# Context keys and values by seven block products per pair of chunks, in a decoder layer in f32

## The chip, the cores and the metric

The kernel runs on one core of a Trainium2 chip. Its metric is the device time of one execution in microseconds, lower is better. The engines are TensorE (PE, matrix products; PEld is its weight load), VectorE (DVE), ScalarE (ACT), GpSimd (POOL) and the queue that issues most transfers (SP). They run side by side, each through its own list of instructions in order, and wait for one another by semaphores.

## The reference

All arrays are f32. `x` has 8 batches of 112 tokens of width 512, the context 8 batches of 375 rows of width 512. Three parts follow one another, each closed by `x = layernorm(x + part(x))`:

```
1. self-attention, 16 heads of 128, causal
2. cross-attention without softmax, 16 heads of 32, f(a) = a + 1 if a > 0 else exp(a):
     q = f(x @ Wq.T);  gate = sigmoid(x @ Wg.T + bg)
     k, v = split(ctx @ Wkv.T);  k = f(k)            # 375 x 512 each, per batch
     summary = sum over context of k v^T;  ksum = sum over context of k
     attn = (q @ summary) / (q . ksum + 1e-6)
     part = (attn * gate) @ Wo.T
3. mixture of 8 experts, top 2 per token, clamped gated unit of width 512
```

The change concerns the line of `k` and `v`: 3000 context rows times a matrix of 512 x 1024.

## The kernel before, in words

The width 512 is cut into `C = 4` blocks of 128 that lie on partitions, and the 896 tokens into 7 tiles of 128. Weights come by 1 MB transfers into nine buffers `slab[0]` to `slab[8]` (three more are added in the last part). PSUM has two groups of four banks, "mm" and "aux"; `bank` hands out the next one, which waits until the last reader of what was in it is done.

**Self-attention** (to 452 us). Per head, `seven` (L279) makes queries and keys of both halves of the tokens with seven block products in place of eight: one accumulator `pa` is read out by ACT three times in the middle of its accumulation (L303, L307, L310), while PE works on another bank. The sums of weights that this needs are made on POOL (L274), where the causal mask of the softmax (L400) runs too.

**Cross-attention** (452 to 748 us). A context of 375 rows is three chunks of `SC = 125`. `load_context` (L690) brings one batch's context, transposed, into one of two buffers `cT`. `project_context(b, sc, n)` (L699) makes the keys (`n = 0`) or values (`n = 1`) of one chunk by four matmuls of 125 x 512 (L704). For keys, DVE takes the minimum with 0 out of PSUM (L713), ACT the exp (L714) and DVE puts the two branches of `f` together (L721); for values, ACT copies them out (L717). `summarize` (L725) sums over the three chunks and masks the result on DVE (L745, L748); `attend` (L751) multiplies with the queries (`dps`, `nps`) and has DVE divide (`z`, with a reciprocal, L768) and multiply into `gate`.

The keys and values of batch 0 are made ahead of the loop, then the queries and gates of all tokens (L789). The loop over batches (L922) makes those of batch `b + 1` while it summarizes batch `b`. Between them it calls `tick` (L667), which moves the open *chains* on by one piece each. A chain is a generator whose `yield` ends a piece: `close(t)` (L866) projects token tile `t` out and adds it (`xops`, L236), normalizes it, and routes it to experts (`x2T`, `lps`, `cps`, scatter into `store`); `keep_scores` (L573) then prepares the tile's first sum (`sTps`, `dbps`, a store into `total`). Within the loop the order of PE, DVE, ACT and SP is the order of the program text; POOL's is planned by the framework, as is everything ahead of the loop. After tile 4 and tile 5 `list_blocks` (L603) makes lists of token blocks for the experts on DVE, and `fetch_weights` / `fetch_tokens` start the transfers for the first steps; step `s` has its weights in slabs `3q` to `3q + 2` with `q = s mod 4`, its biases in `biases[:, q]`.

**Experts** (748 us on). 21 steps of one block of 128 tokens: two products `gups` (L975), sigmoid and clamps, transposes (`aT`, `bT`, L891), one product `yps` (L1001), with weights fetched up to four steps ahead. The chain of tile 6 runs in the first steps.

Of the kernel before, what the change touches and what calls it, by code (L numbers as in the profile page):

```python
# [2 lines left out]

# [6 lines left out]
F32 = mybir.dt.float32  # L10
# [34 lines left out]
def decoder_layer(ctx: ExitStack, tc: tile.TileContext, t_in: dict, out: bass.AP):  # L45
# [182 lines left out]
        nc.scalar.activation(tmp, tmp, AF.Exp)  # L228
        nc.vector.scalar_tensor_tensor(dst, ps, 0.0, tmp, ALU.max, ALU.add)

    def project_and_add(aT, w, tag: str, tiles=range(NT)):

        for t in tiles:
            ps = bank(f"{tag}_{t}")
            for c in range(C):
                nc.tensor.matmul(  # L236
                    ps,
                    aT[:, c, t * P : (t + 1) * P],
                    w[:, c, :],
                    start=(c == 0),  # L240
                    stop=(c == C - 1),
                )
            nc.vector.tensor_add(xn[:, t, :], xn[:, t, :], ps)  # L243
            yield t
# [257 lines left out]
    def route(t: int):  # L502
# [29 lines left out]
            both, expert, i2[:, 1:2], first, ALU.is_equal, ALU.add  # L532
        )
        yield

        cps = bank(f"cps_{t}", "aux")
        nc.tensor.matmul(cps[:, :E], before, both, start=True, stop=True)
# [35 lines left out]
    def keep_scores(t: int, first, both):  # L573

        sco = small.tile([P, E], F32, tag="sco", name=f"sco_{t}")
        yield
        nc.vector.tensor_scalar_mul(sco, both, xe[:, t, XS : XS + 1])
        nc.vector.scalar_tensor_tensor(
            sco, first, xe[:, t, XD : XD + 1], sco, ALU.mult, ALU.add
        )  # L580
        yield
        yield
        sps = bank(f"sTps_{t}", "aux")
        nc.tensor.matmul(sps[:E, :P], sco, ident, start=True, stop=True)
        sT = small.tile([E, P], F32, tag="sT", name=f"sT_{t}", bufs=2)
        nc.scalar.copy(sT, sps[:E, :P])
        yield
        dps = bank(f"dbps_{t}", "aux")
        nc.tensor.matmul(dps, sT, db, start=True, stop=True)  # L589
        first_sum = side.tile([P, D], F32, tag="sum", name=f"sum_{t}")  # L590
        nc.vector.tensor_add(first_sum, xn[:, t, :], dps)
        put = nc.sync.dma_start(out=total[t * P : (t + 1) * P, :], in_=first_sum)
        if t == NT - 1:
            tc.declare_no_dep(put.ins, group="early", reason="tokens of other tiles")
# [81 lines left out]
            tick()  # L676

    with tc.tile_pool(name="cross", bufs=2) as cr:
        wkv = [weights("wkv", 0, 6), weights("wkv", 1, 7)]
        bg = const.tile([P, C], F32, name="bg")  # L680
        nc.sync.dma_start(out=bg, in_=t_in["bg"])
        kv = {}

        values = [
            cr.tile([SC, NSC, C, P + 1], F32, name=f"values{i}", bufs=1) for i in range(2)
# [4 lines left out]
        def load_context(b: int):  # L690
            cT = cr.tile([P, C, SC * NSC], F32, tag="cT", name=f"cT_{b}")
            nc.sync.dma_start(
                out=cT, in_=t_in["ctxT"][b].rearrange("(c p) s -> p c s", p=P)
            )
            kf = cr.tile([SC, NSC, 512], F32, tag="kf", name=f"kf_{b}")
            vs = values[b % 2]
            kv[b] = (cT, kf, vs)

        def project_context(b: int, sc: int, n: int):  # L699

            cT, kf, vs = kv[b]
            ps = bank(f"kvps_{b}_{sc}_{n}")
            for c in range(C):
                nc.tensor.matmul(  # L704
                    ps[:SC, :],
                    cT[:, c, sc * SC : (sc + 1) * SC],
                    wkv[n][:, c, :],
                    start=(c == 0),
                    stop=(c == C - 1),
                )  # L710
            if n == 0:
                tmp = cr.tile([SC, 512], F32, tag="tmp", name=f"kt_{b}_{sc}")
                nc.vector.tensor_scalar_min(tmp, ps[:SC, :], 0.0)  # L713
                nc.scalar.activation(tmp, tmp, AF.Exp)  # L714
                kv[b, sc] = ps, tmp
            else:
                nc.scalar.copy(  # L717
                    vs[:, sc, :, :P], ps[:SC, :].rearrange("p (g e) -> p g e", g=C)
                )
                ps, tmp = kv[b, sc]  # L720
                nc.vector.scalar_tensor_tensor(  # L721
                    kf[:, sc, :], ps[:SC, :], 0.0, tmp, ALU.max, ALU.add
                )

        def summarize(b: int):  # L725

            _, kf, vs = kv[b]
            bdkv = cr.tile([P, C, P], F32, tag="bdkv", name=f"bdkv_{b}")
            bdks = cr.tile([P, C, P], F32, tag="bdks", name=f"bdks_{b}")
            mask = bdmask.unsqueeze(1).broadcast_to([P, 2, P])  # L730
            for i in range(2):
                ps = bank(f"sumps_{b}_{i}", "aux")
                sums = ps[:, : 2 * (P + 1)].rearrange("p (g e) -> p g e", g=2)
                for j in range(2):
                    g = 2 * i + j
                    for sc in range(NSC):
                        nc.tensor.matmul(  # L737
                            sums[:, j, :],
                            kf[:, sc, g * P : (g + 1) * P],
                            vs[:, sc, g, :],  # L740
                            start=(sc == 0),
                            stop=(sc == NSC - 1),
                        )
                pair = slice(2 * i, 2 * i + 2)
                nc.vector.tensor_mul(  # L745
                    bdks[:, pair, :], mask, sums[:, :, P:].broadcast_to([P, 2, P])
                )
                nc.vector.tensor_mul(bdkv[:, pair, :], mask, sums[:, :, :P])  # L748
            return bdkv, bdks
# [20 lines left out]
            nc.vector.tensor_mul(gate[:, :, rows], gate[:, :, rows], z)  # L770

        load_context(0)
        for sc in range(NSC):
            for n in range(2):
                project_context(0, sc, n)
        wxq, wxg = weights("wxq", 0, 4), weights("wxg", 0, 5)
        wxo = weights("wxo", 0, 8)
        xT = keep.tile([P, C, T], F32, tag="xT", name="x1T")
        for _ in transposing(xT, "x1T"):
# [3 lines left out]
        for n, w in (("xq", wxq), ("xg", wxg)):  # L783
            for g in range(C):
                for half in range(2):
# [13 lines left out]
                    else:  # L799
                        nc.scalar.activation(  # L800
                            gate[:, g, cols], ps[:, :HALF], AF.Sigmoid, bias=bg[:, g : g + 1]
                        )
        biases = keep.tile([P, NQ, 2 * I], F32, tag="xT", name="biases")
        blocks = store.rearrange("(n p) w -> n p w", p=P)
        inside = "clamped where it is computed"

# [58 lines left out]

        def close(t: int):  # L866

            for _ in project_and_add(gate, wxo, "xops", (t,)):
                layernorm(t, "ln2")
            yield  # L870
            yield
            first_both = yield from route(t)
            if t == LISTS[0][0] - 1:
                list_blocks(0)
                ahead_w.extend(fetch_weights(s) for s in range(2))
                ahead_x.extend(fetch_tokens(s) for s in range(LISTS[0][1]))
            elif t == LISTS[1][0] - 1:
                list_blocks(1)
                ahead_x.append(fetch_tokens(LISTS[0][1]))
            elif t == NT - 1:  # L880
                list_blocks(2)
            later.append(keep_scores(t, *first_both))
# [33 lines left out]
            st["late"] = s - (STEPS - LATE)  # L916
            return st

        load_context(1)
        ahead_w, ahead_x = [], []  # L920
        in_order = ctx.enter_context(tc.manual_schedule(engines=ORDERED))
        for b in range(B):  # L922
            more = b + 1 < B
            if more:
                project_context(b + 1, 0, 0)
                tick()
            else:
                steps = [start(0, side, "bT")]
                third = fetch_in_parts(2)
                ahead_w.append(next(third))  # L930
                tick()
            sums = summarize(b)
            tick()
            if more:
                project_context(b + 1, 0, 1)
                tick()
            attend(b, *sums, qf, gate)
            tick()
            if more:
                project_context(b + 1, 1, 0)  # L940
                tick()
            if b == LISTS[0][0]:
                chains.append(close(b - 1))
                tick()
            if more:
                project_context(b + 1, 1, 1)
                tick()
            if 0 < b < B - 1 and b != LISTS[0][0]:
                chains.append(close(b - 1))
                tick()  # L950
            if more:
                for n in range(2):
                    project_context(b + 1, 2, n)
                    tick()
            if b + 2 < B:
                load_context(b + 2)


    with tc.tile_pool(name="moe", bufs=2, reuse_waits="tile") as moe:
# [163 lines left out]
        for s in range(STEPS + 1):  # L1123
# [11 lines left out]
            if s + 1 < STEPS:  # L1135
                steps.append(start(s + 1, moe, "bT"))
                if s + 1 > STEPS - LATE:
                    nc.vector.tensor_scalar_mul(diag, ident, keys[:, s + 1 : s + 2])
                if s == 1 or s > STEPS - LATE + 1:
                    tick()  # L1140
                if s == 2:
                    settle(0)
                if s >= 1 and s + 3 < STEPS:
                    ahead_x.append(fetch_tokens(s + 3))
# [85 lines left out]
```

## Time and profile before

| | |
|---|---|
| median of 3 runs | 1013.89 us (1012.16 to 1017.29) |
| the profiled execution's own time | 1014.17 us |
| its span, first to last instruction | 1012.6 us |
| PE / DVE / ACT / POOL busy | 982.3 / 435.2 / 231.8 / 140.9 us |
| granted PE clock | 0.995 |

The page is of one execution. It gives each engine's busy time, the span in 40 slices of 25.3 us (each digit is a share in tenths), the chain of work that ended last, and the costliest groups of instructions: line, engine, operation, output and inputs with shapes, count, then busy us and mean ns of one, then the idle time of the engine ahead of them and what ended it. Other answers of the trace give waits (who waited for whom: us in total, times, longest), the timeline (start us, us, engine, line, operation, the idle time before it in brackets) and the busy time in a stretch. Numbers like L704 are lines of the kernel before.

### The profile page before, as it was taken

The numbers are of one execution on the slowest core, as the hardware profiler recorded it, in microseconds if no ns is written. First come the engines' busy times: TensorE is split into PE (matmuls) and PEld (weight loads), VectorE is DVE, ScalarE is ACT, GpSimd is POOL, SyncE is SP. The second block draws the span as 40 slices with busy tenths as digits, with TensorE's granted clock in tenths as the row PEclk, the third lists the DMA queues.
The fourth block names the chain that finished last, engine by engine and source line by source line (L and its number), as shares of the span: only waits on it lengthen the run. The fifth ranks groups of instructions, "written<-read, shape, count | busy, mean of one in ns | idle before, by whom it ended". The sixth has DMA issues, their size and how long they took to land.

```text
span 1012.6 us, 9328 instructions
## 1 busy us (share of the span) xinstructions
PE 982.3 (97%) x3319; PEld 513.5 (51%) x3319; DVE 435.2 (43%) x988; ACT 231.8 (23%) x406; POOL 140.9 (14%) x183
## 2 busy tenths in 40 slices
PE   7998999999999999999999999999999999999995
PEld 3455544566446655645555555554554444444442
DVE  1356511255124533563314455544676343334384
ACT  1132311133003312312221212122113211121132
POOL 3134200023002211000000000000111212111132
PEclk9999999999999999999999999999999999999998
DMA  8990004111010201110001010111668896692342
GB/s 334 359 347 17 1 1 166 42 42 42 0 42 1 83 0 42 43 61 30 1 0 31 1 63 21 62 42 62 235 264 348 323 388 209 197 342 44 94 95 70
DMA packets 33837, 114.98 MB, mean 114 GB/s; under 512 B 3845, under 2 KB 8005, under 8 KB 26240
## 3 DMA queue, kind: packets, MB, share of 16 engines
q1 hardware_dynamic: 26784, 98.28, 26.4%
q0 software_dynamic: 6336, 15.75, 6.3%
q8 instruction: 26, 0.43, 0.2%
q10 hardware_dynamic: 672, 0.36, 0.1%
q14 instruction: 19, 0.16, 0.0%
HBM read 115.83 MB, written 29.01 MB: 143 GB/s over the span
## 4 chain that ended last, share of the span: by engine, by line
PE 90%; DVE 3%; issue 3%; ACT 1%; DMA 1%; POOL 1%; POOLq 0%; ACTq 0%; DVEq 0%
PE kvps L704 16%; PE gups L975 12%; PE ops L236 10%; PE yps L1001 6%; PE vps L326 6%; PE zps L434 3%; PE xops L236 2%; PE xqps L789 2%; PE xgps L789 2%; PE sps L386 2%; PE sumps L737 2%; PE pps L426 1%; PE dbps L589 1%; PE aT_ps L891 1%; PE bT_ps L891 1%
## 5 line engine op out<-in xcount | busy, mean ns | idle before, releaser
L704 PE MATMUL kvps<-slab,cT 128*125 128x512 f32 x384 | 170.4, 594 | 0.0
L975 PE MATMUL gups<-slab,bT 128*128 128x512 f32 x336 | 151.3, 593 | 0.0
L704 PEld LDWEIGHTS kvps<-slab,cT 128*125 128x125 f32 x384 | 70.4, 188 | 82.9 <-issue 81.3
L236 PE MATMUL ops<-slab,zT 128*128 128x512 f32 x224 | 97.9, 593 | 0.0
L975 PEld LDWEIGHTS gups<-slab,bT 128*128 128x128 f32 x336 | 62.0, 190 | 69.5 <-issue 68.6
L1001 PE MATMUL yps<-slab,aT 128*128 128x512 f32 x168 | 77.6, 606 | 4.1 <-ACT aT L895 4.1
L983 DVE TENSOR_TENSOR gu<-gups,biases 128x512 f32<-128x512 f32 x42 | 29.0, 691 | 118.4 <-PE gups L975 118.3
L236 PEld LDWEIGHTS ops<-slab,zT 128*128 128x128 f32 x224 | 42.0, 190 | 50.3 <-issue 49.3
L326 PE MATMUL vps<-slab,x0T 128*112 128x512 f32 x128 | 59.2, 618 | 1.0 <-DVE x0T L186 0.8
L274 POOL TENSOR_TENSOR ws<-slab 128x256 f32<-128x256 f32 x16 | 11.8, 736 | 316.0 <-PE qk_5c L290 83.0
L562 POOL DMA_INDIRECT store<-xn,rows x14 | 13.8, 985 | 299.6 <-DVE xn L560 242.1
L1001 PEld LDWEIGHTS yps<-slab,aT 128*128 128x128 f32 x168 | 31.9, 194 | 43.4 <-issue 37.6
L1015 POOL DMA_INDIRECT total<-y,nums x19 | 30.4, 1599 | 129.4 <-ACT y L1012 117.5
L713 DVE TENSOR_SCALAR kt<-kvps 125x512 f32<-125x512 f32 x24 | 16.5, 689 | 67.4 <-PE kvps L704 67.4
L243 DVE TENSOR_TENSOR xn<-xn,ops 128x512 f32<-128x512 f32 x28 | 19.2, 686 | 56.1 <-PE ops L236 56.1
L434 PEld LDWEIGHTS zps<-pT,v 112*128 112x128 f32 x256 | 33.5, 192 | 12.3 <-issue 11.2
L326 PEld LDWEIGHTS vps<-slab,x0T 128*112 128x112 f32 x128 | 23.0, 185 | 31.7 <-issue 30.0
L441 DVE COPY zT<-zps 128x448 f32<-128x448 f32 x32 | 20.0, 624 | 39.8 <-PE zps L434 39.8
L434 PE MATMUL zps<-pT,v 112*128 112x112 f32 x256 | 33.4, 273 | 0.0
L714 ACT ACTIVATE kt<-kt 125x512 f32<-125x512 f32 x24 | 15.1, 630 | 78.4 <-DVE kt L713 73.7
L410 DVE TENSOR_REDUCE nm<-p 112x4 f32<-112x448 f32 x32 | 19.7, 616 | 30.8 <-POOL p L400 30.8
L1012 ACT COPY y<-yps 128x512 f32<-128x512 f32 x20 | 11.7, 585 | 92.0 <-issue 81.4
(569 smaller groups left out, 1387.7 us busy)
## 6 DMA issues: line engine op xcount, KB each, us to landing
slab<-in_wg_dram SPq DMA_DIRECT2D x21, 1024.0 KB
slab<-in_wu_dram SPq DMA_DIRECT2D x21, 1024.0 KB
slab<-in_wd_dram SPq DMA_DIRECT2D x21, 1024.0 KB
store<-slab SPq DMA_DIRECT2D x8, 1806.0 KB
biases<-gubs SPq DMA_DIRECT2D x21, 512.0 KB
cT<-in_ctxT_dram SPq DMA_DIRECT2D x8, 750.0 KB
xblk<-store POOLq DMA_DIRECT2D x21, 258.0 KB, 5.4
slab<-in_wq_dram SPq DMA_DIRECT2D x4, 1024.0 KB
```

The lines of the kernel that those rows point to most:

```text
L236: nc.tensor.matmul(ps, aT[:, c, t * P : (t + 1) * P], w[:, c, :], start=(c == 0), stop=(c == C - 1),)
L326: nc.tensor.matmul(ps[:S, :], xT[:, c, b * S : (b + 1) * S], w[:, c, :], start=(c == 0), stop=(c == C - 1),)
L386: nc.tensor.matmul(ps[:S, i * S : (i + 1) * S], qk["q"][:, rows], qk["k"][:, rows], start=True, stop=True,)
L434: nc.tensor.matmul(zps[:, i * S : (i + 1) * S], v[:, half * 4 + i, hl * DH : (hl + 1) * DH], pT[:, i * S : (i + 1) * S], start=True, stop= ...
L704: nc.tensor.matmul(ps[:SC, :], cT[:, c, sc * SC : (sc + 1) * SC], wkv[n][:, c, :], start=(c == 0), stop=(c == C - 1),)
L737: nc.tensor.matmul(sums[:, j, :], kf[:, sc, g * P : (g + 1) * P], vs[:, sc, g, :], start=(sc == 0), stop=(sc == NSC - 1),)
L789: nc.tensor.matmul(ps[:, :HALF], w[:, c, g * P : (g + 1) * P], xT[:, c, cols], start=(c == 0), stop=(c == C - 1),)
L891: nc.tensor.transpose(ps[:, c * P : (c + 1) * P], src[:, c * P : (c + 1) * P], ident)
L975: nc.tensor.matmul(ps, st["bT"][:, c, :], st["w"][k][:, c, :], start=(c == 0), stop=(c == C - 1),)
L983: nc.vector.tensor_add(a, ps, st["bias"][:, k * I : (k + 1) * I])
L1001: nc.tensor.matmul(ps, st["aT"][:, c, :], st["wd"][:, c, :], start=(c == 0), stop=(c == C - 1 and s < STEPS - 1),)
L1015: put = nc.gpsimd.indirect_dma_start(out=total, out_offset=bass.IndirectOffsetOnAxis(ap=st["num"], axis=0), in_=y, in_offset=None, compute ...
```

## The change

Two chunks of context, both split in two halves of the width, are multiplied with the keys' and the values' weights as a 2 x 2 by 2 x 2 block product. Seven products of half the width (two matmuls each) take the place of eight. The chunks are paired 0 with 1 of each batch, and chunk 2 of an even batch with chunk 2 of the next one: 12 pairs. POOL makes four sums of weights once, in slabs 4 and 5, and four sums of context blocks per pair, one pair ahead. The partial results are copied out of `pa` by ACT and added up by DVE. Pairs 0 and 1 are made ahead of the loop; then even batches hold one pair and odd batches two, in three segments each, and batch 7 none. Contexts are loaded one batch further ahead. Step 1's expert weights are fetched at batch 7 instead of after tile 4. The yields of the chains are moved, and `xops` in `close` take a bank of "aux".

```diff
-    def project_and_add(aT, w, tag: str, tiles=range(NT)):
+    def project_and_add(aT, w, tag: str, tiles=range(NT), of="mm"):
...
-            ps = bank(f"{tag}_{t}")
+            ps = bank(f"{tag}_{t}", of)
...
         yield
+        if t < LISTS[1][0] - 1:
+            yield
...
         yield
         yield
+        yield
...
         yield
+        yield
...
         nc.vector.tensor_add(first_sum, xn[:, t, :], dps)
+        yield
+        yield
         put = nc.sync.dma_start(out=total[t * P : (t + 1) * P, :], in_=first_sum)
...
-        wkv = [weights("wkv", 0, 6), weights("wkv", 1, 7)]
+        wk, wv = weights("wkv", 0, 6), weights("wkv", 1, 7)
+
+        wkvs = [
+            slab[i].rearrange("p (a c) n -> p a c n", a=2)[:, a] for i in (4, 5) for a in (0, 1)
+        ]
+        nc.gpsimd.tensor_add(wkvs[0], wv[:, low], wv[:, high])
+        nc.gpsimd.tensor_sub(wkvs[1], wkvs[0], wk[:, low])
+        nc.gpsimd.tensor_sub(wkvs[2], wk[:, low], wv[:, low])
+        nc.gpsimd.tensor_sub(wkvs[3], wk[:, high], wkvs[1])
...
+        pairs = []
+        for b in range(0, B, 2):
+            pairs += [
+                ((b, 0), (b, 1)),
+                ((b, 2), (b + 1, 2)),
+                ((b + 1, 0), (b + 1, 1)),
+            ]
...
+        def prepare_pair(n: int):
+            if n < len(pairs):
+                b11, b12, b21, b22 = blocks_of(n)
+                t = room["sums"][n % 2]
+                nc.gpsimd.tensor_sub(t[:, 0], b12, b11)
+                nc.gpsimd.tensor_sub(t[:, 1], b22, t[:, 0])
+                nc.gpsimd.tensor_sub(t[:, 2], b22, b12)
+                nc.gpsimd.tensor_sub(t[:, 3], b21, t[:, 1])
+
+        def project_pair(n: int):
...
+            def mapped(k, name: str):
+
+                tmp = cr.tile([SC, 512], F32, tag="tmp", name=f"{name}_{n}")
+                nc.vector.tensor_scalar_min(tmp, k, 0.0)
                 nc.scalar.activation(tmp, tmp, AF.Exp)
...
+                nc.vector.scalar_tensor_tensor(k, k, 0.0, tmp, ALU.max, ALU.add)
+
+
+            order = "ab" if n % 2 else "ba"
+            got = {i: bank(f"kvps_{n}{i}")[:SC, :] for i in order + "cd"}
+            pa, pb, pc, pd = (got[i] for i in "abcd")
+            product(pa, b11, wk[:, low], True)
+            nc.scalar.copy(e1, pa)
+            product(pb, b21, wk[:, high], True)
+            nc.vector.tensor_add(k1, e1, pb)
+            if n != 1:
+                prepare_pair(n + 1)
+            yield
+            product(pa, t[:, 1], wkvs[1], False)
+            nc.scalar.copy(e2, pa)
+            product(pc, t[:, 0], wkvs[0], True)
+            nc.vector.tensor_add(k2, e2, pc)
+            mapped(k1, "one")
+            yield
+            product(pa, t[:, 2], wkvs[2], False)
+            nc.scalar.copy(e1, pa)
+            nc.vector.tensor_add(v2, grouped(e1), grouped(pc))
+            product(pd, b22, wkvs[3], True)
+            nc.vector.tensor_add(k2, k2, pd)
+            product(pa, t[:, 3], wv[:, high], False)
+            nc.scalar.copy(v1, grouped(pa))
+            mapped(k2, "two")
...
         load_context(0)
-        for sc in range(NSC):
-            for n in range(2):
-                project_context(0, sc, n)
-        wxq, wxg = weights("wxq", 0, 4), weights("wxg", 0, 5)
+        load_context(1)
+        make_room(
+            slab[3].rearrange("p c n -> p (c n)"), slab[2].rearrange("p c n -> p (c n)")
+        )
+        prepare_pair(0)
+        for n in range(2):
+            for _ in project_pair(n):
+                pass
+        load_context(2)
+        wxq, wxg = weights("wxq", 0, 1), weights("wxg", 0, 0)
...
+        free = biases.rearrange("p q n -> p (q n)")[:, 2 * I :]
+        make_room(free, free[:, 16 * SC :])
...
-            for _ in project_and_add(gate, wxo, "xops", (t,)):
+            for _ in project_and_add(gate, wxo, "xops", (t,), "aux"):
                 layernorm(t, "ln2")
             yield
-            yield
+            if t != LISTS[1][0] - 1:
+                yield
...
-                ahead_w.extend(fetch_weights(s) for s in range(2))
+                ahead_w.append(fetch_weights(0))
...
         for b in range(B):
...
+            if b + 1 < B:
+
+                ns = (3 * b // 2 + 2,) if b % 2 == 0 else (3 * (b + 1) // 2, 3 * (b + 1) // 2 + 1)
+                work = itertools.chain.from_iterable(
+                    itertools.chain(project_pair(n), (None,)) for n in ns
+                )
             else:
+                work = iter(())
                 steps = [start(0, side, "bT")]
+                ahead_w.append(fetch_weights(1))
                 third = fetch_in_parts(2)
                 ahead_w.append(next(third))
-                tick()
+            next(work, None)
+            tick()
             sums = summarize(b)
             tick()
...
+            if next(work, 0) is None:
                 tick()
             attend(b, *sums, qf, gate)
             tick()
...
+            if next(work, 0) is None:
                 tick()
...
+            if 0 < b < B - 1:
                 chains.append(close(b - 1))
                 tick()
...
+            for _ in work:
                 tick()
...
-            if b + 2 < B:
-                load_context(b + 2)
+            if b + 3 < B:
+                load_context(b + 3)
...
-                if s == 1 or s > STEPS - LATE + 1:
+                if s > STEPS - LATE + 1:
                     tick()
```

## The prediction

> **What bounds the kernel now.** I read the page's busy line, slices and chain first, then the group of the changed line, then TensorE's waits from 440 us on, the busy time by stretch, and the timelines of single queues.
>
> ```profile
> PE 982.3 (97%) x3319; PEld 513.5 (51%) x3319; DVE 435.2 (43%) x988; ACT 231.8 (23%) x406; POOL 140.9 (14%) x183
> ...
> PE   7998999999999999999999999999999999999995
> ...
> PEclk9999999999999999999999999999999999999998
> DMA  8990004111010201110001010111668896692342
> ...
> PE kvps L704 16%; PE gups L975 12%; PE ops L236 10%; PE yps L1001 6%; PE vps L326 6%; PE zps L434 3%; PE xops L236 2%; PE xqps L789 2%; PE xgps L789 2%; PE sps L386 2%; PE sumps L737 2%; PE pps L426 1%; PE dbps L589 1%; PE aT_ps L891 1%; PE bT_ps L891 1%
> ...
> L704 PE MATMUL kvps<-slab,cT 128*125 128x512 f32 x384 | 170.4, 594 | 0.0
> ```
>
> TensorE (PE) is busy in every slice but the first and last, and the largest item on the chain is line 704, the one that is changed. Its clock row stands at 9 tenths or more nearly throughout, so there is no slow clock to win back. Each matmul of the program appears as two records (192 in the code, 384 here).
>
> ```profile
> 451.91 20.76 PE L704 MATMUL kvps<-slab,cT 128*125 128x512 f32 x48
> ```
>
> 48 records take 20.60 us from the start of the first to the start of what follows (472.51): 0.429 us a record. The mean of 594 ns overlaps its neighbour and isn't a price.
>
> ```profile
> PE yps L1001 <- ACT aT L895: 4.1, 2, 2.3
> PE dbps L589 <- ACT sT L586: 2.2, 4, 0.7
> PE xops L236 <- DVE again L1089: 1.9, 1, 1.9
> PE sTps L584 <- DVE sco L578: 1.2, 1, 1.2
> PE dps L758 <- DVE bdks L745: 0.5, 1, 0.5
> PE lps L514 <- ACT x2T L510: 0.3, 1, 0.3
> ```
>
> This is all that PE waits from 440 us to the end: 10.2 us, none for a transfer. So a product removed is time removed, as long as these waits don't grow. VectorE (DVE) and ScalarE (ACT) have room on average:
>
> ```profile
> sum 224.00, PE 220.45 PEld 119.91 DVE 111.58 ACT 49.84 POOL 11.49; mean PE 220.45 PEld 119.91 DVE 111.58 ACT 49.84 POOL 11.49
> ```
>
> (busy us of each engine in 524 to 748, the loop over batches.) Half of DVE is free there, but in pieces.
>
> [...] from 713 to 719 us a chain of small routing operations on DVE stands ahead of the masks of `summarize`, and PE waits for them (the 0.5 us above). [...] The query/key projection already does so:
>
> ```profile
> 45.38 0.53 ACT L307 COPY slab<-qk_0a 128x448 f32<-128x448 f32 x1 [2.47 <-PE qk_0a L290]
> ```
>
> PE runs qk_0c from 45.18 and returns to qk_0a at 46.68 without a wait: one product hides the copy. [...] The trace has 1.28 us[...] (a load from 574.78 is followed by its exp at 576.08). [...]
>
> **Products removed.** Before: 24 chunks x 8 matmuls = 192. After: 12 pairs x 7 products x 2 = 168, of the same 125x512 shape. 24 x 2 records x 0.429 us = 20.6 us less on PE. Ahead of the loop there is more (two pairs, 24.0 us, for three chunks, 20.6); the loop loses the rest.
>
> **Work added beside PE.** Rows:
>
> ```profile
> L713 DVE TENSOR_SCALAR kt<-kvps x24: 682/692/692, 455.5 to 737.6; 125x512 f32<-125x512 f32 x24
> L721 DVE SCALAR_TENSOR_TENSOR kf<-kvps,kt x24: 683/692/692, 458.3 to 740.3; 125x512 f32<-125x512 f32 x24
> L717 ACT COPY values<-kvps x24: 586/586/590, 459.0 to 741.0; 125x512 f32<-125x512 f32 x24
> ...
> L985 DVE TENSOR_SCALAR gu<-gu x21: 426/427/454, 758.0 to 986.7; 128x512 f32<-128x512 f32 x21
> ...
> L274 POOL TENSOR_TENSOR ws<-slab 128x256 f32<-128x256 f32 x16 | 11.8, 736 | 316.0 <-PE qk_5c L290 83.0
> ...
> L768 DVE RECIPROCAL z<-z 128x448 f32<-128x448 f32 x7 | 20.7, 2953 | 0.2
> ```
>
> DVE: four additions a pair, 48 x 0.69 = 33.1 us; the 24 minima now read SBUF (0.43 for 0.69, as L985), -6.2: +27 us. ACT: four copies a pair for two, 24 x 0.59 = +14 us. POOL: four sums a pair of 250 elements, 4 x 0.74 = 2.9 us, twelve times, and four weight sums of 1024, 4 x 0.74 each: +47 us. In the loop DVE gets about 22 us more in 24 us less: 134 of 200. None becomes the bound by its sum; order decides.
>
> **The new waits.** In a pair the accumulator `pa` is copied out by ACT three times before PE may add to it again (`e1`, `e2`, `e1`), each covered by one other product, 1.72 us, against 0.2 (PE to ACT, seen throughout) + 0.59: 0.9 us to spare if ACT is free. Behind a waiting copy on ACT stand exp, square root and the other copies; PE itself waits, so all that follows. I walked the in-order queues over the loop with the durations above; the same walk of the kernel before puts its first `gups` 223.4 us after the start of the loop, where the trace has 748.05 - 523.84 = 224.2, but counts 13.6 us of waits where the trace has 10.2.
>
> In batches 3 and 5 the first copy of the second pair is late. Counted from the end of `dps`, PE has 0.89 (`nps`) + 5.15 (three products) + 0.37 (`cps`) + 3.43 (`xops`) + 3.43 = 13.3 us until it needs that copy. It stands on ACT behind the square root of `layernorm`. DVE until then, after a 0.5 us tail: 0.69 (map) + 0.69 (`sum`) + 1.4 (top two) + 4.9 (`z`, with the 2.95 reciprocal) + 1.4 (two additions) + 1.9 (map, with exp) + 1.9 (routing) + 1.6 (`xn` and its statistics), together 15.0 with the tail, less some 0.3 where two overlap; then 0.4 for the root and 0.7 for the copy: 15.8. PE waits **2.5 us, twice**. In batches 1, 3 and 5 the last `pa` waits 0.5 for a copy behind an exp with its table load. Batch 1's `summarize` waits 1.7 for the last keys of the pair before.
>
> At batch 7 two things meet: `list_blocks(0)` (4.2 us on DVE, 715.28 to 719.4 before) now falls into the short batch 6 of one pair, and `x2T` of tile 5 comes three instructions after its `xops`. From `dps` of batch 6 PE has 10.2 us until `x2T`, and DVE has 15.6 to go to the end of the layernorm: **5.4 us**. The sigmoid of step 0 is late behind the same backlog, with `bT` behind it on ACT: 4.1. All waits: 17.7, against the walk's 13.6 for before. By the walk the change costs 4.1 us; scaled by traced to walked, 3.1; against the traced 10.2, 7.5. I take 4, ends 0 and 10.
>
> Ahead of the loop: the last keys stand on DVE before the copies of `x1T` (0.5 us), an exp with a table load before a copy (0.5): 1. The weight sums on POOL can land before a causal mask at 397 us whose result PE takes 0.8 us after it is ready: 0 to 3, I take 0, since POOL is idle from 361 to 394. `prepare_pair` is issued a pair (12 us) ahead, 2.9 us of work; contexts come a batch ahead. I cost both at nothing; if POOL sat behind a late scatter, the second product would wait up to that delay.
>
> **Loads and ticks.** Step 1's weights move from 721 us (below) to the end of the last pair, since slabs 4 and 5 hold weight sums; `biases` is shared too.
>
> ```profile
> 723.38 0.33 SPq L834 DMA_DIRECT2D slab<-in_wd_dram  x1
> ...
> 720.00:748.00 28.00, 27.71 (x120) 16.11 (x120) 16.07 (x44) 6.62 (x11) 1.69 (x3) 1.00 0.97 390
> ```
>
> At 390 GB/s step 0 (3.67 MB), step 1 (3.67) and two slabs and a bias of step 2 (2.62) need 25.5 us. Step 0 starts some 5.6 us ahead of the end of the last product; step 1 is complete 13 us after it, step 2's part 20; PE gets to step 1's first product after 22 without any wait. So nothing is added; SP's `total` stores move behind two ticks and block no load that is near due. Token block 0 lands by the walk (put, then 5.4 us) 0.5 us ahead of its transposes: 0 to 2. `xops` in "aux", the further yields and the dropped tick cost nothing beyond the walk.
>
> **Sum.** -20.6 + 4 + 1 = -15.6 us. The profiled execution took 1014.17 us (span 1012.6), which gives 998.6. The median of the runs is 0.3 lower: **998.3 us**.
>
> **Rivals.** (1) ACT's copies become the beat of every pair. 36 waits (three a pair) are new; if each ends 0.57 us late the 20.6 us are gone, from 0.71 us it is slower by over 0.5%, which is about what a measurement of this kernel can tell from no change. A table load (1.28) ahead of each copy, less 0.9 to spare, is only 0.4; DVE must be behind as well. At 0.9 each: 1013.9 - 20.6 + 32.4 = 1026. For it: strict order, and the 2.5 us above. Against: qk's same pattern, free of waits in nearly all heads. 6%. (2) The loads after batch 6 come at half the rate, as in slice 35 (197 GB/s): step 1 is complete 32 us after the last product, 10 late: 1008. 8%. (3) The waits of DVE are hidden better than walked, and those of before shrink too: -20.6 - 4: 989. 12%. (4) DVE's order costs twice what I walked, or the POOL sums hit the mask: 1005. 14%. My forecast: 60%. That the products aren't fewer can't be; the diff counts them.
>
> **Range.** The forecast's ends are 1013.9 - 20.6 + 0 = 993 and + 10 + 1 = 1004; with rivals 3 and 4: 990 to 1007. Faster by over 0.5% (below 1008.8): 88%; within 0.5%: 6%; slower: 6%.
>
> **What would show it.** Line 704's successor with 336 records and 144 us of chain; DVE near 462 us, ACT 246, POOL 188; PE's waits from the loop on 13 to 18 us, with products waiting for copies of `e1` in batches 3 and 5 and `x2T` or `gups` around batch 7; no PE wait for a transfer. Waits for ACT in every pair, or for `slab`, would prove me wrong.

## The result, and the profile after

The changed kernel takes 999.53 us (median of 4 runs, 998.96 to 1001.35) where the kernel before takes 1014.26: a ratio of 0.9856 (95% interval 0.9827 to 0.9884), 14.7 us less. The forecast was 998.3, range 990 to 1007. The profiled execution after has a span of 997.4 us, 15.2 less than before. Line numbers from here on are those of the changed kernel unless an experiment's own lines are shown; `product` is line 758.

Of the page after, the rows that answer to those shown of before:

```profile
PE 963.8 (97%) x3271; PEld 505.1 (51%) x3271; DVE 462.5 (46%) x1036; ACT 244.7 (25%) x430; POOL 185.2 (19%) x235
...
PE   7998999999999999999999999999899999999994
...
PEclk9999999999999999999999999999999999999998
```

PE has 48 records fewer, the 24 matmuls; DVE, ACT and POOL are busy 27, 13 and 44 us longer, as the prediction had it (27, 14, 47). One slice of PE (the 29th of 40, 698 to 723 us) shows an 8 where before has a 9. All waits of PE from 440 us to the end (total, times, longest), in the same view as before:

```profile
PE xops L237 <- DVE gate L845: 2.6, 1, 2.6
PE yps L1080 <- ACT aT L979: 2.3, 1, 2.3
PE x2T_ps L508 <- DVE xn L222: 2.2, 1, 2.2
PE gups L1054 <- ACT bT L979: 2.0, 1, 2.0
PE sumps L812 <- DVE kf L772: 1.8, 1, 1.8
PE xops L237 <- DVE sco L580: 0.6, 1, 0.6
PE xops L237 <- PE kvps_3a L758: 0.6, 1, 0.6
PE kvps_10a L758 <- ACT biases L779: 0.2, 1, 0.2
```

The sum is 12.3, against 10.2 before and the 13 to 18 of the prediction, but it lies elsewhere: 8.0 of it in the loop over batches, where before had 3.6. No wait is for a transfer, and only the last row is for one of the new copies. From here each kernel's loop is measured from its first product after the queries and gates to its first `gups`. The granted clock, as a list of stretches in the trace, adds what the page's tenths hide: twice in the loop, from 615.46 and from 721.27 us, it is at one half for 3.413 us. The trace of before has no such stretch in its loop. Busy times by stretch, with the clock as the third number from the end:

```profile
612.00:616.00 4.00, 4.00 (x22) 2.63 (x21) 2.48 (x6) 1.52 (x2) 1.50 (x2) 0.93 0.00 0
616.00:620.00 4.00, 4.00 (x13) 2.56 (x12) 3.83 (x8) 0.00 (x0) 0.00 (x0) 0.64 0.18 68
...
721.00:724.00 3.00, 2.44 (x3) 1.18 (x4) 2.49 (x6) 0.41 (x1) 0.00 (x0) 0.55 1.04 345
```

PE is busy throughout 616 to 620 us, at 0.64 of its clock. From `dbps` to `xops` it needs 11.0 us in this batch (3) and 9.4 us for the same work in batch 5, where the clock is whole: such a stretch costs about half of its length, 1.7 us, and shows in no view of waits.

The two spans, cut at the same points (us):

| | before | after | change |
|---|---|---|---|
| to the first product | 451.9 | 452.8 | +0.9 |
| products ahead of the loop | 20.6 | 24.2 | +3.6 |
| x1T, queries, gates | 51.2 | 51.2 | 0 |
| loop | 224.4 | 209.0 | -15.4 |
| first `gups` to the start of the last | 238.1 | 235.4 | -2.7 |
| from there to PE's end | 16.0 | 14.4 | -1.6 |

### The profile page after: what moved, and what is told of

Read it like the earlier page. It is cut to its first block, busy times and chain, and to the rows that moved or that the text cites. A ratio compares the mean times of both kernels' runs of the same rounds, so it can differ in the third digit from the quotient of the medians.

```text
span 997.4 us, 9419 instructions
## 1 busy us (share of the span) xinstructions
PE 963.8 (97%) x3271; PEld 505.1 (51%) x3271; DVE 462.5 (46%) x1036; ACT 244.7 (25%) x430; POOL 185.2 (19%) x235
## 4 chain that ended last, share of the span: by engine, by line
PE 86%; DVE 7%; issue 3%; ACT 1%; POOL 1%; DMA 1%; SPq 0%; POOLq 0%; DVEq 0%; ACTq 0%
PE gups L1054 13%; PE ops L237 10%; PE yps L1080 6%; PE vps L327 6%; PE zps L435 3%; PE xqps L870 2%; PE xgps L870 2%; PE sumps L812 2%; PE sps L387 2%; PE xops L237 2%; DVE z L843 1%; PE pps L427 1%; PE aT_ps L975 1%; PE bT_ps L975 1%; DVE p L412 1%
## 5 line engine op out<-in xcount | busy, mean ns | idle before, releaser
L435 PEld LDWEIGHTS zps<-pT,v 112*128 112x128 f32 x256 | 33.5, 192 | 12.3 <-issue 11.2
L237 PE MATMUL xops<-slab,gate 128*128 128x512 f32 x56 | 27.3, 632 | 3.8 <-DVE gate L845 2.6
L1066 ACT ACTIVATE sg<-gu 128x512 f32<-128x512 f32 x21 | 13.2, 630 | 71.2 <-DVE gu L1064 53.6
L395 ACT ACTIVATE p<-sps 112x448 f32<-112x448 f32 x32 | 17.4, 544 | 45.6 <-PE sps L387 45.6
L387 PE MATMUL sps<-k,q 128*112 128x112 f32 x256 | 28.0, 262 | 0.0
```

Source lines behind the costliest of these rows:

```text
L237: nc.tensor.matmul(ps, aT[:, c, t * P : (t + 1) * P], w[:, c, :], start=(c == 0), stop=(c == C - 1),)
L387: nc.tensor.matmul(ps[:S, i * S : (i + 1) * S], qk["q"][:, rows], qk["k"][:, rows], start=True, stop=True,)
L435: nc.tensor.matmul(zps[:, i * S : (i + 1) * S], v[:, half * 4 + i, hl * DH : (hl + 1) * DH], pT[:, i * S : (i + 1) * S], start=True, stop= ...
```

## The experiments

**My theory after reading both traces:** the products are saved in full; in the loop DVE's order, made longer by the additions, takes part of it back at `xops` and `sumps`; the copies on ACT and the sums on POOL cost little. **Rivals:** the copies are the beat; the schedule, not the products, brings the gain.

**1. Eight products in the new schedule (e1).** `project_pair` computes the same four chunks by eight plain products; the four sums of weights and `prepare_pair` are gone.

```diff
-            product(pa, b11, wk[:, low], True)
-            nc.scalar.copy(e1, pa)
-            product(pb, b21, wk[:, high], True)
-            nc.vector.tensor_add(k1, e1, pb)
...
+            product(pa, b11, wk[:, low], True, False)
+            product(pa, b21, wk[:, high], False, True)
...
```

> Everything stays as after (pairs across batches, contexts a batch earlier, ticks, slabs), but each pair is computed by eight plain products again: 192 matmuls, no copies of pa, no additions, no sums of blocks or weights on GpSimd. My theory: the gain is the removed matmuls, 24 x 0.858 = 20.6 us; of it some 3 us are lost again to waits and slow clock that the fuller DVE makes, so this kernel takes 1013 to 1019 us, centre 1016, DVE near 435 us, and the waits of TensorE in the loop are 2 to 6 us where after has 8. Rival (the schedule brings the gain, by filling waits of the loop): under 1008. Rival (the waits cost much more than I read in the trace): over 1020 can't be, since then after would have lost more than it did; 1010 or less would say that waits of over 10 us go away with the additions.

Measured: 1010.35 us (1009.93 to 1010.71), 0.9959 of before (0.9944 to 0.9975), so 3 to 9 us less than I expected and just above what the rivals name (1010, 1008). The schedule alone brings 4 us, and the seven products the other 10 (0.9959 to 0.9856), half of the 20.6 us of work that they save. Most of the other half goes in after's loop, to 5.3 us more of waits and 1.7 more of half clock than here (account below). The waits of this kernel, same view:

```profile
PE yps L1065 <- ACT aT L965: 2.3, 1, 2.3
PE x2T_ps L508 <- DVE xn L222: 2.2, 1, 2.2
PE gups L1039 <- ACT bT L965: 2.0, 1, 2.0
PE xops L237 <- DVE gate L832: 0.6, 1, 0.6
```

Where those 4 us come from: its loop (218.1 us) is 6.3 shorter than that of before, for 8 matmuls that moved ahead of it (6.9 us), so no gain there. But from the first `gups` to PE's end it takes 249.8 us, as after does (249.9), where before takes 254.2. So the last two rows of the table above don't come from the seven products. The first of them belongs to the schedule and is mostly waits: before has `xops` of tile 6 (1.9), `dbps` (0.7) and a `yps` (1.8) in the first steps, after and this kernel have one `gups` (2.0). The second is a half-clock stretch of 3.413 us at 995.9 in the trace of before. It isn't the schedule's: the traces of 5, 7 and 9 below, with the new schedule, have one there as well (980 to 987 us), and all stand at a wait for the last `yps` of 2.3 to 2.6 us, which after and this kernel have too without one.

**2. The copies twice (e2).** Each of the three copies of `pa` in a pair is issued twice.

```diff
             nc.scalar.copy(e1, pa)
+            nc.scalar.copy(e1, pa)
```

> After, with each of the 36 copies of pa into e1 or e2 made twice in a row (the same result), so that each ends 0.59 us later. My theory: one product of 1.72 us covers 0.2 + 0.59, so 0.9 us were to spare and 0.3 still are; only the copies that are late already (batches 3 and 5) show: 999 to 1003 us, no wait of a product for ACT in most pairs. Rival 1 of the prediction (the copies are the beat of every pair): 36 x 0.59 = 21 us more, 1018 to 1022.

Measured: 998.14 us (997.05 to 1002.03), 0.9849 (0.9826 to 0.9873), 0.9 us below my range. As in the theory, two products wait for a copy, 0.9 us each, in batches 3 and 5, and no others:

```profile
PE kvps_7a L758 <- ACT biases L780: 0.9, 1, 0.9
PE kvps_10a L758 <- ACT biases L780: 0.9, 1, 0.9
```

The copies are not the beat. What I had not expected: the wait of `sumps` in batch 1 fell from 1.8 to 0.4. In after, ACT's load of the exp table at 539.08 waits for DVE's minimum and the exp follows at 540.37; here the load starts at 537.68, right behind the copy, and is over when the minimum arrives. See 5.

**3. The listing later (e3).** In batch 6, `list_blocks(0)` is issued two ticks later, while `keep_scores` opens where it did.

```diff
             if t == LISTS[0][0] - 1:
+                later.append(keep_scores(t, *first_both))
+                yield
+                yield
                 list_blocks(0)
```

> After, with list_blocks(0) issued two ticks later in batch 6, behind the z chain of attend on DVE instead of ahead of it. Theory A (xops of tile 5 needs the gate of batch 6, which stood behind 4.05 us of listing): the 2.56 us wait of xops is gone, and with the idle time the half-clock stretch that follows it (1.7 us); 1.5 to 4.5 us less than after, 995 to 998. Theory B (DVE's whole backlog is the limit until x2T of tile 5, its order matters little): the wait comes back at x2T, which grows from 2.2 to some 3 to 5 us, and the time is 998 to 999.5. If the token block of step 0 comes too late (the list feeds its address), bT of step 0 waits and the time is 1000 to 1003.

Measured: 1003.37 us (1003.30 to 1003.74), 0.9893 (0.9878 to 0.9908). The wait of `xops` for the gate is gone (it starts at 719.57 us, right behind the products): theory A is right about its cause. But the address of the token block comes out of that list, and `bT` of step 0 then waits for the block: the issue went from 714.40 to 724.22 us and the block was there at 731.

```profile
PE bT_ps L979 <- DMA xblk<-store: 7.8, 1, 7.8
```

The third outcome decided, just above its range.

**4. The slabs of `wk` and `wv` exchanged (e4).**

```diff
-        wk, wv = weights("wkv", 0, 6), weights("wkv", 1, 7)
+        wk, wv = weights("wkv", 0, 7), weights("wkv", 1, 6)
```

> After, with the slabs of wk and wv exchanged (7 and 6 for 6 and 7), so that the first sum of weights on GpSimd, which needs wv alone, can't start before the later slab lands near 387 us. Theory: the sum at 329.5 us made DVE's addition p<-p,nm take 2.64 us for 0.63, hence the 1.5 us wait of qk_11a; that row is back near 0.63 us, the wait is gone, and the time is 1 to 1.5 us less than after, 998.0 to 998.5. Rival (the row was slow for another reason, such as the transfer of the slab into SBUF): row and wait stay, 999.5. Four sums in a row end 2.4 us later than now; if that meets the causal mask of the next head, up to 1 us is lost there.

Measured: 998.66 us (995.97 to 999.17), 0.9840 (0.9824 to 0.9856). The timelines of POOL and DVE in after, then DVE's in this kernel:

```profile
329.52 2.35 POOL L691 TENSOR_TENSOR slab<-slab 128x1024 f32<-128x1024 f32 x1
```

```profile
329.71 2.64 DVE L412 TENSOR_TENSOR p<-p,nm 112x448 f32<-112x448 f32 x1
```

```profile
329.55 0.63 DVE L412 TENSOR_TENSOR p<-p,nm 112x448 f32<-112x448 f32 x1
```

With POOL idle the same addition takes 0.63 us; with POOL's sum begun 0.2 us ahead of it, it ends 0.5 us after that sum. What holds it up is not shown beyond that. The 1.5 us wait of `qk_11a` is gone; four sums in a row (385.18 to 394.6) make `qk_14a` wait 0.6 instead. The gain of 0.9 us in waits is below what the times can tell.

**5. The tables ahead (e5).** A one-column exp or sigmoid on a constant stands ahead of the awaited one.

```diff
+                if name == "one" and n % 3 != 1:
+                    nc.scalar.activation(probe[:, 1:2], probe[:, 0:1], AF.Exp)
                 nc.scalar.activation(tmp, tmp, AF.Exp)
...
+                if s in (0, STEPS - 1):
+                    nc.scalar.activation(probe[:, 1:2], probe[:, 0:1], AF.Sigmoid)
                 nc.scalar.activation(sg, a, AF.Sigmoid, scale=ALPHA)
```

> After, with a one-column exp ahead of the exp of the first map of a pair (two pairs in three), and a one-column sigmoid ahead of the sigmoid of the first and the last step; both work on a constant, so that ACT's table is switched before the awaited input is there. Theory: at three places the 1.28 us load itself stood behind DVE (539.08, 747.68 and 973.59 us in the trace of after) and PE waited behind it; the waits of sumps (1.8), gups (2.0) and the last yps (2.3) each shrink by some 1.2 us: 3 to 4 us less than after, 995.5 to 996.5. Rival (DVE, not the load, is last there, as at x2T): the waits stay, 999 to 1000.

Measured: 998.43 us (995.30 to 998.57), 0.9847 (0.9828 to 0.9866); the interval holds the ratio of after. ACT's timeline at step 0, after and then this kernel:

```profile
747.68 1.28 ACT L1066 ACT_TABLE_LOAD   x1 [5.82 <-DVE gu L1064]
748.98 0.63 ACT L1066 ACTIVATE sg<-gu 128x512 f32<-128x512 f32 x1
```

```profile
741.07 1.28 ACT L1071 ACT_TABLE_LOAD   x1
742.36 0.20 ACT L1071 ACTIVATE probe<-probe 128x1 f32<-128x1 f32 x1
746.89 0.63 ACT L1072 ACTIVATE sg<-gu 128x512 f32<-128x512 f32 x1 [4.32 <-DVE gu L1068]
```

In after ACT is idle for 5.8 us and then loads the table when the input is there. Loaded ahead, the wait of `gups` falls from 2.0 to 0.7 and that of `sumps` from 1.8 to 0.4, as expected. That of the last `yps` doesn't fall (2.3 to 2.6), so its cause is another one (8). This execution has three half-clock stretches ahead of its end (92.75, 720.80 and 980.22 us) where after has two, which hides 1.7 of the 2.6 us gained at those two waits; one run of the five, 995.30, has a mean clock of 0.995 for 0.992. So the waits are shorter, as shown, but the median is above my range (995.5 to 996.5).

**6. The additions of the keys left out (e6).** The kernel leaves out three of the four additions of a pair, so its keys are only part of the product.

```diff
-            nc.vector.tensor_add(k1, e1, pb)
-            nc.vector.tensor_add(k2, e2, pc)
-            mapped(k1, "one")
+            mapped(k1, pb, "one")
-            nc.vector.tensor_add(k2, k2, pd)
-            mapped(k2, "two")
+            mapped(k2, pd, "two")
```

> After, leaving out the three additions of each pair that make the keys (the map reads the parts pb and pd alone, so keys are only part of the product); seven products, three copies and GpSimd's sums stay. Theory: DVE's additions, not the copies or GpSimd, cost the loop its 5 us of new waits at xops and sumps. Without them the loop (209.0 us from its first product to the first gups in after) takes 203.5 to 205.5, xops waits under 1 us, DVE is busy some 21 us less, and the time is 994 to 996. Rival (the copies or GpSimd's sums make the loss): the loop stays at 208 to 209, 998.5 to 999.5.

Measured: 994.20 us (992.63 to 995.91), 0.9816 (0.9794 to 0.9838). DVE is busy 18 us less, and the loop takes 202.6 us, 6.4 less than in after, with the copies and POOL's sums in place: 3.6 us of waits, 1.7 for one half-clock stretch that is not there, and 1.1 that is neither. `sumps` and two of the three `xops` no longer wait. The one of batch 6 still waits 2.2; the listing stands ahead of the gate there, and PE has one product less in that batch than in experiment 1, where it waits 0.6. Of the 5.3 us of waits in the loop that after has over experiment 1, the additions make 3.6.

**7. The third chunk alone (e7).** 176 matmuls, the same work in each batch.

```diff
-                ns = (3 * b // 2 + 2,) if b % 2 == 0 else (3 * (b + 1) // 2, 3 * (b + 1) // 2 + 1)
-                work = itertools.chain.from_iterable(
-                    itertools.chain(project_pair(n), (None,)) for n in ns
-                )
+                work = itertools.chain(project_third(b + 1), project_pair(b + 1))
```

> After, with the third chunk of each batch projected by itself in eight matmuls, ahead of the batch's one pair, instead of being paired with the third chunk of the next batch: 176 matmuls for 168, each batch with the same work. Theory: 8 x 0.858 = 6.9 us more on PE, but no short batches, so the waits of xops (3.8 us in all) and of sumps (1.8) are mostly gone: 1000 to 1003, that is 1 to 3 us slower than after. Rival 1 (short batches cost nothing beyond their waits in other places): 1005 to 1007. Rival 2 (the short batches cost more than their waits): under 999.

Measured: 1005.82 us (1005.61 to 1006.23), 0.9931 (0.9912 to 0.9950): rival 1's number, but not by its reason.

```profile
PE bT_ps L990 <- DMA xblk<-store: 3.8, 1, 3.8
PE kvps_7a L754 <- ACT biases L788: 3.5, 1, 3.5
```

`xops` waits 1.5 us in all and `sumps` not at all. But in batch 6 the listing now begins at 719.00 instead of 709.54 us: the layernorm of tile 5 stands behind it on DVE, the root on ACT waits for DVE, a copy of `pa` stands behind that root, and PE waits for the copy. The token block comes later too. This is the mechanism that the prediction had put into batches 3 and 5. The even batches as such are not at fault, and the place of the listing confounds this experiment as a test of pairing.

**8. X_EPS on ACT, alone (e10) and with the rest (e8, e11).** One addition of `attend` moves from DVE to ACT. A second kernel has it together with 4 and 5, and a third also puts the copy of the last `aT` ahead of the two roots on ACT.

```diff
-            nc.vector.tensor_scalar_add(zf, dps[:, : C * S], X_EPS)
+            nc.scalar.activation(zf, dps[:, : C * S], AF.Copy, bias=X_EPS)
```

> After, with the addition of X_EPS in attend on ACT instead of DVE, and nothing else. Theory: DVE's chain from dps to gate is 0.62 us shorter in each batch, so the waits of xops (0.6, 0.6 and 2.6) become 0, 0 and 1.9, and the loop is 1.5 to 3 us shorter: 996.5 to 998. Rival (ACT's queue delays the addition by what DVE saves): loop and time as after, 999 to 1000.

> After, with the slabs of wk and wv exchanged (e4), the tables switched ahead (e5), and the addition of X_EPS in attend moved from DVE to ACT. Theory: 3 to 4 us from the tables, 0.9 from the exchange, 1 to 3 from 0.62 us less on DVE's chain ahead of each gate: 991.5 to 994.5. If ACT's queue is the later one at that addition, the last part is zero or negative: 994.5 to 997.

> e8, with the copy of the last aT on ACT ahead of the two roots of the closing normalization that stood before it. Theory: the last yps waits for a root that waits for DVE, not for its sigmoid; its wait falls from 2.6 us to some 0.8, and the half clock after it goes with it: 988.5 to 990.5 us. Rival (the wait is the sigmoid's): 991.5 to 992.5.

Measured: alone 992.26 us (991.66 to 997.96), 0.9801 (0.9776 to 0.9826); 4, 5 and this together 992.02 (991.40 to 992.80), 0.9793 (0.9777 to 0.9810); with the third edit **989.87 us** (989.39 to 990.60), 0.9764 (0.9751 to 0.9778), faster than both kernels. The last two are within their ranges, the first is 4 us below its own. Waits of the single edit from 520 us on:

```profile
PE yps L1080 <- ACT aT L979: 2.3, 1, 2.3
PE x2T_ps L508 <- DVE xn L222: 2.2, 1, 2.2
PE xops L237 <- DVE gate L845: 1.9, 1, 1.9
PE gups L1054 <- ACT bT L979: 1.6, 1, 1.6
PE sumps L812 <- DVE kf L772: 0.9, 1, 0.9
```

0.62 us off DVE in each batch takes 6.8 us off the loop (202.2): two waits of 0.6 are gone, the others shrink, together 3.0; and no half-clock stretch falls into this loop, 3.4 more. The waits alone are at the upper end of what I had expected (1.5 to 3), and the rest is the clock, which isn't shown to be this edit's gain: the stretch at 615 us is absent from the traces of 2, 4 and 5 too, and the third kernel, with the same wait of 1.9 at `xops`, has a stretch behind it (716.13). One of the five runs (997.96) has a mean clock of 0.990 for 0.997. In the third kernel the roots are behind the last `yps`:

```profile
PE yps L1086 <- ACT aT L983: 0.8, 1, 0.8
```

It waited 2.6 us in the second, which shows that the roots, and DVE's statistics ahead of them, were its wait.

**9. `dbps` a tick earlier (e9).**

```diff
         nc.scalar.copy(sT, sps[:E, :P])
         yield
-        yield
...
+        yield
         put = nc.sync.dma_start(out=total[t * P : (t + 1) * P, :], in_=first_sum)
```

> After, with dbps one tick earlier and the store of its sum still where it was, so that in batches 3 and 5 it no longer stands together with lps, dps and nps. Theory: [...] the stretch at 615 us followed dbps, lps and dps, which are small. With dbps elsewhere no half-clock stretch follows there, in the profile, though one may still follow the idle time at 719 to 721 us; against that dbps may wait 0.5 us for its copy on ACT, as in the kernel before: 998 to 1000.5. Rival: such stretches come anywhere at random; then one stands inside the loop at some place where PE was fully busy with large matmuls.

Measured: 1003.57 us (1002.24 to 1003.72), 0.9897 (0.9881 to 0.9913), 3 us above my range. The first wait from 520 us on:

```profile
PE xops L237 <- DVE gate L845: 5.7, 4, 2.9
```

No half-clock stretch stands near 615 or 671 us. That decides nothing: the traces of 2, 4, 5, 6 and 10, where `dbps` is as in after, have none there either. But at the end of the loop, where this edit puts `dbps` ahead of `lps` and `dps`, a stretch of 6.83 us follows (737.33), as one of 3.413 follows these three in after (615.46). The loss is elsewhere: in after, `dbps` (1.05 us on PE) stood between the product of `pc` and `dps`, and covered DVE's map ahead of `z`; in batch 5 the gate was there at 682.73 us and `xops` began at 682.79. Without it PE reaches `xops` 1 us earlier and waits 1.0, 0.7 and 1.0 us for the gate in batches 3, 4 and 5 too. PE's waits in the loop come to 11.2 us for 8.0, the half clock to 1.5 for 3.4, and the loop is 2.0 us longer. The rest of the loss in this execution is half clock outside it, at 92.2 and 986.5 us and in the second part of the stretch from 737.33.

**The account of the loop.** The rest is the loop, less PE's waits in it, less half of its half-clock stretches (us):

| | loop | waits | half clock | rest |
|---|---|---|---|---|
| before | 224.4 | 3.6 | 0 | 220.8 |
| eight products (1) | 218.1 | 2.7 | 1.7 | 213.7 |
| after | 209.0 | 8.0 | 3.4 | 197.6 |
| no additions of keys (6) | 202.6 | 4.4 | 1.7 | 196.5 |
| X_EPS on ACT (8) | 202.2 | 5.0 | 0 | 197.2 |

The rest falls by 7.1 from before to 1 (8 matmuls moved, 6.9) and by 16.1 from 1 to after (20 matmuls removed from the loop, 17.2). The products are saved all but 1 us; waits and clock take 7.8 us more than before.

## Why the prediction was right, and what it had wrong

The number was right (999.5 for 998.3), and so was the main term; several of the others were not, and they cancel. That they do so to 1.2 us is luck.

- **Products, -20.6:** held. +3.6 ahead of the loop for +3.4, and some -23.2 for -24.0 in it (table above).
- **Busy times:** held within 3 us for all three engines. "Order decides" held as well (6, 8 and 9).
- **Waits, net +4:** from 440 us on they grew by 2.1 (12.3 for 10.2), within the ends 0 and 10; the loop's grew by 4.4, those after it shrank by 2.4. As a sum of 17.7 walked us it was wrong, and so are most single terms. The 1.7 at `summarize` was 1.8. The two waits for `e1` of 2.5 us were 0 and 0.2, the later `pa` waits of 0.5 did not appear, `x2T` was 2.2 for 5.4, `gups` 2.0 for 4.1. For `e1` the step that failed is the start of the walk, the tail, map and `sum` (1.9 together) after the end of `dps`. The lines of batch 5:

```profile
672.35 1.28 ACT L771 ACT_TABLE_LOAD   x1
674.59 0.63 ACT L771 ACTIVATE one<-one 125x512 f32<-125x512 f32 x1 [0.96 <-DVE one L770]
675.86 0.68 DVE L596 TENSOR_TENSOR sum<-xn,dbps 128x512 f32<-128x512 f32 x1
676.28 1.06 PE L833 MATMUL nps<-qf,bdkv 128*128 128x112 f32 x8
```

  When PE is done with `dps` (676.28), DVE is already within `sum` and needs only 0.2 us more. The table load started as soon as the copy before it was done and was over when DVE's minimum arrived, so DVE was 1.3 us earlier than with a load behind the minimum. The other steps held: 1.3 (top two), 4.9 (`z`), 1.3 (additions), 1.7 (map), 1.9 (routing), 1.6 (statistics). Batch 3 is alike (load at 611.61); that it waits 0 goes with PE's half clock there, since it waits 0.2 in 4 and 5, which have none. At batch 0 and step 0 the load does wait.
- **A wait that the walk lacked:** it took the gates of the batches before to be enough for `xops`. Tile `t` has 128 tokens and a batch 112, so tile `b - 1` reaches into batch `b`, and `xops` needs that batch's gate too. DVE's queue in batch 6 of after:

```profile
713.50 0.17 DVE L667 TENSOR_TENSOR taken<-got,taken 128x8 f32<-128x8 f32 x1
713.59 0.68 DVE L788 TENSOR_TENSOR kf<-biases,kvps_11c 125x512 f32<-125x512 f32 x1
...
716.51 0.62 DVE L842 TENSOR_SCALAR z<-dps 128x448 f32<-128x448 f32 x1
717.16 2.95 DVE L843 RECIPROCAL z<-z 128x448 f32<-128x448 f32 x1
720.22 0.62 DVE L844 TENSOR_TENSOR z<-z,nps 128x448 f32<-128x448 f32 x1
720.88 0.62 DVE L845 TENSOR_TENSOR gate<-gate,z 128x448 f32<-128x448 f32 x1
```

  The listing ends at 713.6, PE is done with its products at 719.0, the gate is there at 721.5: the 2.6 us at `xops`, part of what the prediction had put at `x2T`. It was right that the listing and the short batch meet, and a place too late.
- **Weight sums on POOL, 0 to 3, taken 0:** 1.5 us of wait, within the bounds. The prediction argued from POOL's idle time at 361 to 394 us; the sum that needs `wv` alone came at 329.5, and it hit DVE's queue, not POOL's.
- **Clock:** "there is no slow clock to win back" was read as a constant. Two new stretches cost 3.4 us in the loop of after.
- **What follows the loop** was taken to stay as it was, but for `gups`. It is 2.7 us shorter by the schedule, 2.4 of it waits, and 1.6 by a half-clock stretch that the trace of before has there (1).
- **Ahead of the loop, 1 (x1T copies, table load):** not seen. **Loads, token block, `prepare_pair`, yields at 0:** no wait of PE for a transfer, and with POOL's sums and ACT's copies in place the rest of the loop (196.5 in 6) is that of 1 less the products (213.7 - 17.2), so they cost nothing there that can be seen. The token block has little room: 9.8 us later it cost 7.8 (3).
- **Rivals.** 1 fell by experiment 2: twice the copies cost two waits of 0.9. 2 fell by the absence of any wait for a transfer; slower loads were not tried. 3 and 4 each hold in part and cancel: the waits after the loop shrank, those of DVE and the clock cost more.

## What to carry to other kernels

When a change saves work on the engine that bounds and adds some to one that is half idle, follow the longest chain of the second engine to the next instruction of the first that needs it, with every operand of that instruction looked up: here 0.62 us off such a chain in each batch took 3.0 us of waits off the loop. An account by stretches (work, waits, clock) between fixed points tells a saving from its losses, where a sum that fits may be two errors that cancel. Ask of each late activation whether its table load waits as well; a one-column activation on a constant loaded it while the engine was idle (at 741.07 us for 747.68; 2.6 us off two waits in 5, though the times don't clearly show it).

## What the runs showed of the hardware

- **Half-clock stretches, as the traces list them.** 3.413 us from 615.46 and from 721.27 in after and from 995.91 in before, 6.83 us from 737.33 in 9, 10.24 us in 3; after and before also end in one (from 990.93 and 1006.15). Some stand at a wait of PE: the one at 721.27 starts 0.3 us ahead of the end of the 2.6 us at `xops`, the one at 995.91 0.1 us ahead of the end of the 2.3 us at the last `yps`, and the one of 10.24 comes after 7.8 us of waiting. Waits as long come without one too: after waits 2.3 us for the last `yps`, and 3.0 us in the attention (`qk_3a`, to 91.70), where experiment 1 waits the same 3.0 us and a stretch follows (91.96). What decides was not shown.
- **A stretch can come without any wait.** In five places one follows `dbps`, `lps` and `dps` back to back (615.46 in after, where the three take PE 1.05, 0.91 and 1.03 us from 612.62 on; 671.26 in the second kernel of 8). This order stands 21 times in the traces; the other 16 have no stretch behind them. Why, no run here shows.
- **Half clock goes with most of the scatter between the runs of before.** Of nine runs of the kernel before, taken together, two have a mean clock of 0.997 and 0.998 and took 1011.8 and 1012.4 us (those of experiments 1 to 4); seven have 0.994 or 0.995 and took 1014.1 to 1015.0.
- **One table load, two prices.** 1.28 us when it waits together with its activation (539.08 us in after), nothing when it goes ahead (672.35). What decides between them in the emitted order was not settled.
